# The prologue of a two-layer graph network on one core: degree count, row statistics and scaling in another order, with small operations moved between engines

## The chip, the cores and the metric

The kernel runs on one core of a Trainium2 chip. The metric is the time on the device in microseconds (us), from the first to the last instruction and what lies around them. Timed runs are given as a median; one further execution was taken with the hardware profiler, and everything that is said of single instructions comes from that one.

## The reference

`x` has 12,500 rows of 256 float32 values; an edge list of 200,000 pairs (`src`, `dst`) is sorted by `dst`. Two blocks follow one another:

```python
h = relu(layernorm(x))                       # mean and variance of each row
# block 1: two graph convolutions on the edges and a loop at every node
deg  = segment_sum(1, dst) + 1
dinv = rsqrt(deg)
conv(h, W, b) = segment_sum((h @ W)[src] * dinv[src] * dinv[dst], dst) + b
x = x + relu(conv(relu(conv(h @ W_pre + b_pre, W1, b1)), W2, b2)) @ W_post + b_post
# block 2: an attention layer in which node n mixes four heads of row dst[n]
x = x + attention(relu(layernorm(x)))
```

Because the weights can be multiplied after the sum over edges, the kernel gathers rows `relu(layernorm(x)) * dinv`, sums them by `dst`, and multiplies the sums by `W_pre @ W1`.

## The kernel before

Everything that runs is in `fast_path` (L414); `general_path` is a fallback for edge lists that are far from even, and is branched over here. Instructions keep the order in which the program emits them, engine by engine: there is no planner that moves them, so an instruction that waits holds back all that was emitted behind it on its engine. Semaphores are made by the language from the tiles that are read and written.

The 98 tiles of 128 rows (`NT`) are handled in 14 groups of seven (`NG`, `G`). The program has four stages.

**The prologue** (L506 to L870) makes `table1` in device memory: the rows `relu((x - mean) * rstd) * dinv`, with `dinv` in column 256. Its parts are:

- `load_edges` (L534) brings `dst` and `src` into 112 partitions of 1792 edges, `load_x` (L560) one group of x (896 KB). Eleven groups have buffers of their own (`XB`); the last three take the buffers of groups 0 to 2 once these have been written out (L823).
- The weights are multiplied on the PE (L670 to L688), and ACT copies each product out of PSUM.
- `near`, the offset of each `dst` within its neighbourhood, is made on DVE (L619), turned on the PE and copied out by ACT as `near_t` (`turned`, L699). `to_t` and `src_t` are made in the same way from `fto_f` (L634, L719) and `fsrc_f` (L723).
- `mean`, `off`, `ok` and `keeps` (L645 to L667) are a dozen one-column operations on POOL and one on DVE. They check that the edges are even enough and give the offsets of the later sums.
- The degree count runs over 16 blocks, four, four, four, three and one for the five parts `k`. `count_block` (L728) makes a one-hot `hot_r` on DVE (two buffers) and counts it with small matmuls. At the end of a part, `place` (L746) copies the counts (ACT, L750), makes a second one-hot `hot_n` (DVE, L753), multiplies both (PE, L759), copies the result (ACT, L773) and spreads it over partitions (PE, L778, 16 matmuls).
- `stats` (L781) takes mean and variance of a group: seven `bn_stats`, seven `bn_aggr` on DVE, one square root on ACT.
- `norms` (L790) turns the degrees of a part into `dinv`, and makes for all its rows the scale `sc` and the shift `nb` on DVE. Parts hold 3, 3, 4, 3 and 1 groups.
- `scale` (L806) writes one group in place, seven ACTIVATEs on ACT, or, with `both`, four on ACT and three pairs of operations on DVE; POOL copies `dinv` into column 256 (L810); SP starts the write to `table1` (L821).

What sets the order is the loop at L828: each block is followed by the statistics of the next group, then `place`, `norms` of the part before and one `scale` where they are due. After the loop the last groups are scaled with `both`.

**The first convolution** (`convolve`, L920, called at L1127) gathers 1563 tiles of 128 edges with indirect DMAs that POOL issues (L1077), and sums them on the PE with one-hots (L1082). **The second convolution** (L1235) does the same with `table2`. **The attention** (L1245 on) gathers its rows and writes the output. None of the three is touched by the change.

Of the kernel before, what the change touches and what calls it, by code (L numbers as in the profile page):

```python
# [413 lines left out]
def fast_path(  # L414
# [91 lines left out]
    with tc.tile_pool(name="fprep", bufs=1) as prep:  # L506
# [26 lines left out]

        def load_edges(e, pad, name):  # L534
            t = prep.tile([NCH, CE], I32, name=name)
# [24 lines left out]
        def load_x(g):  # L560
            n0, n1 = g * G * P, min((g + 1) * G * P, N)

            xt = prep.tile([P, G, D1], F32, name="fxt", bufs=XB)
# [11 lines left out]
        for g in range(XB):  # L575
            load_x(g)
            if g == 1:
                src_r = load_edges(src, 0, "fsrc_r")
# [39 lines left out]
        near = prep.tile([NCH, CE], F32, name="near_f")  # L618
# [9 lines left out]
        for k, q in enumerate(Q):  # L628
# [4 lines left out]
        to_f = prep.tile([NCH, CE], F32, name="fto_f")  # L633
        nc.vector.tensor_scalar(to_f, dst_r, base, None, op0=ALU.subtract)  # L634

# [6 lines left out]

        mean = prep.tile([NCH, 1], F32, name="fmean")  # L645
        nc.gpsimd.iota(mean, pattern=[[0, 1]], base=-LAG, channel_multiplier=M,
                       allow_small_or_imprecise_dtypes=True)
        nc.gpsimd.tensor_scalar(mean, mean, 0.0, None, op0=ALU.max)
        mean_i = prep.tile([NCH, 1], I32, name="mean_i")
        nc.gpsimd.tensor_copy(mean_i, mean)  # L650
        nc.vector.tensor_scalar(mean_i, mean_i, ~(P - 1), None, op0=ALU.bitwise_and)
        off = prep.tile([NCH, 1], F32, name="off")
        nc.gpsimd.tensor_copy(off, mean_i)
        nc.gpsimd.tensor_scalar(off, off, float(P * NT), None, op0=ALU.min)
        nc.gpsimd.tensor_sub(off, base, off)


        ok = prep.tile([NCH, 2], F32, name="ok")
        nc.gpsimd.tensor_sub(keeps[:, 1:2], mean, base)
        nc.gpsimd.tensor_scalar(keeps[:, 0:1], keeps[:, 1:2], 0.0, None, op0=ALU.is_le)  # L660
        nc.gpsimd.tensor_scalar(keeps[:, 1:2], keeps[:, 1:2], float(NL), float(P), op0=ALU.add,
                                op1=ALU.min)
        nc.gpsimd.tensor_scalar(ok[:, 0:1], off, 0.0, None, op0=ALU.is_ge)
        nc.gpsimd.tensor_scalar(ok[:, 1:2], off, float(OFF), None, op0=ALU.is_le)
        for i in range(2):
            nc.gpsimd.tensor_mul(keeps[:, 0:1], keeps[:, 0:1], ok[:, i:i + 1])
        nc.gpsimd.tensor_scalar(off, off, 0.0, float(OFF), op0=ALU.max, op1=ALU.min)  # L667
# [22 lines left out]
        with tc.tile_pool(name="fpsum", bufs=2, space=PSUM) as psum, \  # L690
# [28 lines left out]
            turned(to_f, to_t.rearrange("p c j -> p j c"), by_act)  # L719
            src_f = prep.tile([NCH, CE], F32, name="fsrc_f")  # L720

            def turn_src():
                nc.scalar.activation(src_f, src_r, AF.Copy)  # L723
                turned(src_f, src_t.rearrange("p c j -> p j c"), by_act)
# [21 lines left out]
            def place(k):  # L746
# [4 lines left out]
                hot = prep.tile([I, L * max(AW)], BF16, name="hot_n", bufs=2)  # L751
                hot = hot[:rows, :L * aw].rearrange("i (l a) -> i l a", a=aw)
                nc.vector.tensor_tensor(hot, a_bf[:rows, k, :, None].to_broadcast([rows, L, aw]),  # L753
                                        iota_a[:rows, :, :aw], ALU.is_equal)
# [26 lines left out]
            def stats(g):  # L781
                w0 = g * G
                st = prep.tile([P, G, 6], F32, name="fstats", bufs=2)
                for i in range(G):
                    nc.vector.bn_stats(st[:, i, :], xs[g][:, i, :D])
                for i in range(G):
                    nc.vector.bn_aggr(mv[:, w0 + i, :], st[:, i, :])
# [573 lines left out]
```

## Time and profile before

| what | us |
|---|---|
| median of 3 timed runs | 4939.63 (4938.75 to 4964.09) |
| the profiled execution, its own time | 4244.97 |
| its span, first to last instruction | 4243.1 |
| start to first gather of the first convolution | 126.47 |
| first to last gather of the second convolution | 2106.23 to 4070.28 |
| POOL busy, PE busy, DVE busy, ACT busy over the span | 3102.3, 3275.7, 1116.3, 409.1 |

The profiled execution took 694.7 us less than the median of the timed runs. Busy times are sums over the span; the timeline gives the start and length of each instruction or run of like instructions, with the engine's idle time before it and what ended it in brackets. Lines of the profile name an instruction by engine, source line, operation, and output and input tiles.

### The profile page before, as it was taken

What the parts mean: (1) busy time and instruction counts of PE and PEld (TensorE: products, weight loads), DVE (VectorE), ACT (ScalarE), POOL (GpSimd) and SP (SyncE); (2) the same over time, 40 slices, a digit from 0 to 9 for tenths busy, and PEclk for the clock granted to TensorE, in tenths of its full rate; (3) what the DMA queues carried; (4) which work ended last, traced back from release to release, by engine and by line L of the source; (5) the groups of instructions that cost most, each with busy time, mean ns of one, the idle gap of its engine ahead of it and who ended that gap; (6) DMA issues with size and microseconds to landing.
All of it is one profiled execution on the core that took longest, in us unless ns stands there. A gap on an engine that the chain in (4) does not pass through costs nothing. (4 is left out here: it accounts for less than half of the span.)

```text
span 4243.1 us, 32312 instructions
## 1 busy us (share of the span) xinstructions
PE 3275.7 (77%) x10867; PEld 2000.0 (47%) x10867; DVE 1116.3 (26%) x2257; ACT 409.1 (10%) x1066; POOL 3102.3 (73%) x3304
## 2 busy tenths in 40 slices
PE   6587878877887788788678877777878877877773
PEld 5244444434444444444345545555555554555552
DVE  8322222122222222222122222222222222222238
ACT  4100000000000000000001111111111111111122
POOL 2677777777777777777677777777777777777766
PEclk7678787788777777877778898998788888888886
DMA  6544444444444444444445444444444444444456
GB/s 212 159 121 119 119 119 121 119 118 120 121 119 119 119 121 119 119 119 120 124 124 135 127 123 124 127 124 123 124 126 125 124 124 126 126 123 124 124 157 186
DMA packets 300154, 543.46 MB, mean 128 GB/s; under 512 B 83149, under 2 KB 198604, under 8 KB 299980
## 3 DMA queue, kind: packets, MB, share of 16 engines
q0 software_dynamic: 153520, 414.27, 36.7%
q1 hardware_dynamic: 115014, 111.19, 8.4%
q10 hardware_dynamic: 31446, 15.83, 1.3%
q8 instruction: 90, 1.47, 0.1%
q14 instruction: 84, 0.69, 0.1%
HBM read 488.00 MB, written 52.93 MB: 127 GB/s over the span
## 5 line engine op out<-in xcount | busy, mean ns | idle before, releaser
L1077 POOL DMA_INDIRECT fgot<-ftable,fsrc_t x3126 | 2978.4, 953 | 985.1 <-issue 954.1
L1082 PE MATMUL facc<-fgot,fhot 128*128 128x257 f32 (+1 forms) x6252 | 2365.7, 496 | 788.6 <-DMA fgot<-ftable,fsrc_t 749.8
L1082 PEld LDWEIGHTS facc<-fgot,fhot 128*128 128x128 f32 x6252 | 1215.9, 228 | 1798.4 <-DMA fgot<-ftable,fsrc_t 1462.9
L1028 DVE TENSOR_TENSOR buf<-buf,fturn 128x256 f32 x224 | 94.5, 422 | 1677.4 <-PE fturn L972 1645.0
L1005 DVE TENSOR_TENSOR fhot<-iota_p,to_t 128x1792 f32<-128x1792 f32 x224 | 448.3, 2003 | 0.1
L1166 DVE SCALAR_TENSOR_TENSOR fx<-fpo,fdinv,fxb 128x256 f32<-128x256 f32 x97 | 47.0, 484 | 1301.5 <-PE fpo L1162 1301.5
L1012 ACT ACTIVATE fsums<-facc 128x257 f32<-128x257 f32 (+1 forms) x224 | 86.4, 386 | 1352.3 <-PE facc L1082 1348.5
L1111 PE MATMUL fpo<-wf,buf 128*128 128x256 f32 x388 | 157.6, 551 | 0.4 <-DVE buf L1028 0.4
L1149 PE MATMUL fpz<-buf,fwb 128*128 128x128 f32 x776 | 145.1, 316 | 0.0
L1272 POOL DMA_INDIRECT fal<-table_l,fsrc_t x98 | 94.8, 967 | 50.9 <-issue 27.4
L1111 PEld LDWEIGHTS fpo<-wf,buf 128*128 128x128 f32 x388 | 114.9, 297 | 29.3 <-DVE buf L1028 0.7
L1149 PEld LDWEIGHTS fpz<-buf,fwb 128*128 128x128 f32 x776 | 120.3, 219 | 14.9 <-issue 2.9
L1116 ACT ACTIVATE fo<-fpo,fdinv 128x256 f32<-128x256 f32 x97 | 46.0, 474 | 791.7 <-PE fpo L1112 791.7
L972 PE MATMUL fturn<-fident,self 128*128 128x128 f32 x396 | 87.8, 309 | 35.5 <-DMA self<-ftable 33.7
L1161 PE MATMUL fpo<-fwo,fz 128*128 128x256 f32 x388 | 111.2, 411 | 0.0
L1151 PE MATMUL fpz<-rm,fb2r 1*128 1x128 f32 x388 | 102.0, 345 | 0.0
L972 PE MATMUL fturn<-fident,fsums 128*128 128x128 f32 x448 | 99.5, 309 | 0.5 <-ACT fsums L1012 0.5
L1263 PE MATMUL fends<-rows,hot_t 128*128 128x260 f32 x196 | 68.6, 526 | 38.9 <-ACT fxg L1265 38.7
L1044 DVE COPY buf<-buf 128x640 f32<-128x640 f32 x194 | 97.6, 503 | 3.3
L972 PEld LDWEIGHTS fturn<-fident,fsums 128*128 128x128 f32 x448 | 72.8, 163 | 34.4 <-issue 11.5
L1112 PE MATMUL fpo<-bb,fins 2*128 2x256 f32 x194 | 86.1, 530 | 0.0
L972 PEld LDWEIGHTS fturn<-fident,self 128*128 128x128 f32 x396 | 58.8, 164 | 43.9 <-issue 35.7
(205 smaller groups left out, 1590.0 us busy)
## 6 DMA issues: line engine op xcount, KB each, us to landing
fgot<-ftable,fsrc_t POOLq DMA_INDIRECT x3126
ftable<-fxt SPq DMA_DIRECT2D x14, 910.0 KB
self<-ftable SPq DMA_DIRECT2D x97, 130.0 KB
ftable<-fo ACTq DMA_DIRECT2D x98, 128.0 KB
kept_x<-fx SPq DMA_DIRECT2D x98, 128.0 KB
fxr<-kept_x SPq DMA_DIRECT2D x14, 896.0 KB
self<-ftable SPq DMA_DIRECT2D x97, 128.0 KB
fxb<-in_x_dram SPq DMA_DIRECT2D x97, 128.0 KB
```

Source lines behind the costliest of these rows:

```text
L972: nc.tensor.transpose(v["pt"][:, i * KC + k, :], rows[:, k * P:(k + 1) * P], ident)
L1005: nc.vector.tensor_tensor(h[:, :n, :], iota_p[:, None, :].to_broadcast([P, n, P]), to_t[:, c, :n, None].to_broadcast([P, n, P]), ALU.is_equal)
L1012: nc.scalar.activation(sb, acc, AF.Copy)
L1028: nc.vector.tensor_add(b, b, v["pt"][:, :KC, :])
L1044: nc.vector.tensor_copy(nxt[:, :, :BW - P], buf[:, :, P:])
L1077: nc.gpsimd.indirect_dma_start(out=got, out_offset=None, in_=table[:], in_offset=bass.IndirectOffsetOnAxis(ap=src_t[:, c, j:j + 1], axis=0))
L1082: nc.tensor.matmul(acc, hots[c][:, j, :], got[:, :width], start=(j == 0), stop=(j == nj[c] - 1))
L1111: nc.tensor.matmul(po, buf[:, k, :P], wf[:, k, :], start=(k == 0), stop=False)
L1149: nc.tensor.matmul(pz[:, m, :], wb[:, k, m * P:(m + 1) * P], buf[:, k, :P], start=(k == 0), stop=False)
L1151: nc.tensor.matmul(pz[:, m, :], b2r[:, m * P:(m + 1) * P], v["rm"], start=False, stop=True)
L1161: nc.tensor.matmul(po, v["z"][:, m, :], wo[:, m, :], start=(m == 0), stop=False)
L1272: nc.gpsimd.indirect_dma_start(out=al[:, i, :], out_offset=None, in_=table_l[:], in_offset=bass.IndirectOffsetOnAxis(ap=src_t[:, c, j:j + ...
```

## The change

All of it is in the prologue:

- Statistics of one group follow only every second block of the degree count (and group 0's come first, ahead of the weight products); the last five groups' statistics follow the loop, each with the scaling of one group.
- The reciprocal of a group's standard deviation is taken per group (`flip`), between the `bn_stats` and the `bn_aggr` of the next group.
- The scale `sc` and the shift `nb` are made per group of seven columns on POOL, inside `scale`, with three operations; before, DVE made them per part with two.
- `deg` is copied out of PSUM by ACT, not DVE.
- The second one-hots `hot_n` of all five parts are made on POOL ahead of the loop, each by a subtraction and a comparison with zero.
- `to_f` and its turning move from before the loop to behind the first block.
- Groups 11 to 13 of x get a pool of their own in the place of the edge rows, and are loaded once `src` has been turned (behind block 1), not when a written group gives its buffer.
- The block of `mean`, `off`, `ok`, `keeps` moves from ahead of the weight products to behind the scaling, ahead of the gathers.
- `norms` is due two blocks after its `place`; while the loop and the rounds of statistics run, `scale` uses ACT alone; `both` is left for groups that remain after that.

```diff
+        edges = ExitStack()
+        rows_p = edges.enter_context(tc.tile_pool(name="frows", bufs=1))
-            t = prep.tile([NCH, CE], I32, name=name)
+            t = rows_p.tile([NCH, CE], I32, name=name)
...
-        to_f = prep.tile([NCH, CE], F32, name="fto_f")
-        nc.vector.tensor_scalar(to_f, dst_r, base, None, op0=ALU.subtract)
...
-        mean = prep.tile([NCH, 1], F32, name="fmean")
-        nc.gpsimd.iota(mean, pattern=[[0, 1]], base=-LAG, channel_multiplier=M,
-                       allow_small_or_imprecise_dtypes=True)
...
+        flipped = set()
+        def flip(g):
+            if g not in flipped:
+                flipped.add(g)
+                nc.vector.reciprocal(sc[:, g * G:(g + 1) * G], sc[:, g * G:(g + 1) * G])
+        def stats(g):
+            w0 = g * G
+            st = prep.tile([P, G, 6], F32, name="fstats", bufs=2)
+            for i in range(G):
+                nc.vector.bn_stats(st[:, i, :], xs[g][:, i, :D])
+            if g:
+                flip(g - 1)
+            for i in range(G):
+                nc.vector.bn_aggr(mv[:, w0 + i, :], st[:, i, :])
+            nc.scalar.activation(sc[:, w0:w0 + G], mv[:, w0:w0 + G, 1], AF.Sqrt, bias=eps)
+        stats(0)
         with tc.tile_pool(name="wpsum", bufs=2, space=PSUM) as psum:
...
-            turned(to_f, to_t.rearrange("p c j -> p j c"), by_act)
-            src_f = prep.tile([NCH, CE], F32, name="fsrc_f")
+            hot_n = []
+            for k, q in enumerate(Q):
+                h = prep.tile([I, L * max(AW)], BF16, name="hot_n", bufs=NPT)
+                h = h[:J * q, :L * AW[k]].rearrange("i (l a) -> i l a", a=AW[k])
+                nc.gpsimd.tensor_sub(h, iota_a[:J * q, :, :AW[k]],
+                                     a_bf[:J * q, k, :, None].to_broadcast([J * q, L, AW[k]]))
+                nc.gpsimd.tensor_scalar(h, h, 0.0, None, op0=ALU.is_equal)
+                hot_n.append(h)
+            def turn_to():
+                to_f = rows_p.tile([NCH, CE], F32, name="fto_f")
+                nc.vector.tensor_scalar(to_f, dst_r, base, None, op0=ALU.subtract)
+                turned(to_f, to_t.rearrange("p c j -> p j c"), by_act)
...
-                nc.vector.tensor_tensor(hot, a_bf[:rows, k, :, None].to_broadcast([rows, L, aw]),
-                                        iota_a[:rows, :, :aw], ALU.is_equal)
+                hot = hot_n[k]
...
-                nc.vector.tensor_scalar(deg[:, w0:w1], parts[k][:, :w1 - w0], 1.0, None,
-                                        op0=ALU.add)
+                nc.scalar.activation(deg[:, w0:w1], parts[k][:, :w1 - w0], AF.Copy, bias=1.0)
                 nc.scalar.activation(root[:, w0:w1], deg[:, w0:w1], AF.Sqrt)
-                nc.vector.reciprocal(sc[:, w0:w1], sc[:, w0:w1])
                 nc.vector.reciprocal(dinv[:, w0:w1], root[:, w0:w1])
-                nc.vector.tensor_mul(sc[:, w0:w1], sc[:, w0:w1], dinv[:, w0:w1])
-                nc.vector.scalar_tensor_tensor(nb[:, w0:w1], mv[:, w0:w1, 0], -1.0, sc[:, w0:w1],
-                                               op0=ALU.mult, op1=ALU.mult)
...
+                ws = slice(g * G, (g + 1) * G)
+                flip(g)
+                nc.gpsimd.tensor_mul(sc[:, ws], sc[:, ws], dinv[:, ws])
+                nc.gpsimd.tensor_mul(nb[:, ws], mv[:, ws, 0], sc[:, ws])
+                nc.gpsimd.tensor_scalar(nb[:, ws], nb[:, ws], -1.0, None, op0=ALU.mult)
...
-                if g + XB < NG:
-                    load_x(g + XB)
-            stats(0)
+            n_stats, due = 1, []
             for s, (k, j0) in enumerate(blocks):
                 count_block(k, j0)
-                if s + 1 < NG:
-                    stats(s + 1)
+                if s % 2 == 0:
+                    stats(n_stats)
+                    n_stats += 1
                 if j0 + JB[k] >= J:
                     place(k)
-                if k and (j0 == JB[k] or JB[k] >= J):
-                    norms(k - 1)
+                    due.append((s + 2, k))
+                if due and due[0][0] == s:
+                    norms(due.pop(0)[1])
+                if s == 0:
+                    turn_to()
                 if s == 1:
                     turn_src()
-                if to_scale:
-                    scale(k == NPT - 1)
-            norms(NPT - 1)
+                    edges.close()
+                    more = edges.enter_context(tc.tile_pool(name="fmore", bufs=1))
+                    for g in range(XB, NG):
+                        load_x(g, more)
+                if to_scale and to_scale[0] < n_stats:
+                    scale(False)
+            while n_stats < NG or due:
+                if n_stats < NG:
+                    stats(n_stats)
+                    n_stats += 1
+                if due:
+                    norms(due.pop(0)[1])
+                if to_scale and to_scale[0] < n_stats:
+                    scale(False)
             while to_scale:
                 scale(True)
             nc.vector.reciprocal(dinv2, deg)
+        edges.close()
+        mean = prep.tile([NCH, 1], F32, name="fmean")
...
```

## The prediction

> **What bounds the kernel now.** I read the page's groups first, then busy times by stretches of 20 us, then the timelines of all engines up to the first gather. The chain of waits reaches back only some 20 us from the end, and says nothing here.
>
> From the page, the group of the gathers:
>
> ```profile
> L1077 POOL DMA_INDIRECT fgot<-ftable,fsrc_t x3126 | 2978.4, 953 | 985.1 <-issue 954.1
> ```
>
> The 3126 gathers of both convolutions take (2978.4 + 985.1)/3126 = 1.27 us each, back to back. POOL's issue paces everything behind the first gather, and the change touches nothing there. So the change is worth what it does to the time of the first gather. POOL's timeline:
>
> ```profile
> 107.53 0.20 POOL L810 COPY fxt<-fdinv 128x7 f32<-128x7 f32 x1 [3.36 <-DVE fdinv L798]
> 126.47 1.24 POOL L1077 DMA_INDIRECT fgot<-ftable,fsrc_t  x1 [18.75 <-issue]
> ```
>
> The first gather waits for the last write of the first table. The stretches (columns: stretch, its length, then busy us and count of PE, PEld, DVE, ACT, POOL, then granted clock, DMA share, GB/s) show who sets that:
>
> ```profile
> 20.00:40.00 20.00, 15.64 (x86) 12.19 (x86) 20.00 (x73) 8.92 (x16) 1.51 (x9) 0.63 1.09 352
> 40.00:60.00 20.00, 12.63 (x79) 10.30 (x79) 19.71 (x63) 8.62 (x21) 0.19 (x1) 0.74 0.15 52
> 60.00:80.00 20.00, 13.90 (x79) 11.63 (x79) 19.71 (x63) 11.93 (x29) 1.36 (x9) 0.72 0.64 188
> 80.00:100.00 20.00, 15.45 (x102) 13.15 (x103) 15.98 (x37) 13.78 (x34) 0.59 (x4) 0.67 0.70 229
> 100.00:120.00 20.00, 6.80 (x36) 5.18 (x34) 14.06 (x50) 13.67 (x31) 0.66 (x4) 0.50 0.74 249
> ```
>
> DVE is full from 20 to 90 us; PE is at two thirds to three quarters beside it; POOL has nothing to do. From DVE's timeline, its one long wait and the first count block behind it:
>
> ```profile
> 18.94 0.15 DVE L651 TENSOR_SCALAR mean_i<-mean_i 112x1 int32<-112x1 int32 x1 [4.03 <-POOL mean_i L650]
> ...
> 21.78 2.00 DVE L734 TENSOR_TENSOR hot_r<-near_t,iota_r 128x3584 bf16<-128x3584 bf16 x1
> ```
>
> From PE's, counting at two speeds (16 matmuls each) and the last count:
>
> ```profile
> 53.84 3.15 PE L742 MATMUL tiles<-hot_r,slide 128*56 128x224 bf16 x16 [3.66 <-DVE hot_r L734]
> ...
> 74.50 2.09 PE L742 MATMUL tiles<-hot_r,slide 128*56 128x224 bf16 x16 [1.19 <-DVE hot_r L734]
> ...
> 102.05 0.57 PE L759 MATMUL count<-hot_n,tiles_b 14*32 14x55 bf16 x7 [0.50 <-ACT tiles_b L750]
> ```
>
> From ACT's, the last scalings, and from SP's, the last writes and the read that waits for them:
>
> ```profile
> 107.07 9.92 ACT L819 ACTIVATE fxt<-fxt,fnb,fsc 128x256 f32<-128x256 f32 x20
> ```
>
> ```profile
> 79.86 38.21 SPq L821 DMA_DIRECT2D ftable<-fxt  x11
> 125.60 6.94 SPq L966 DMA_DIRECT2D self<-ftable  x4
> ```
>
> The last count ends at 102.6, ACT and DVE together scale the last groups until 117.5, the last write starts at 117.7 and has landed by 125.6. That is the path: DVE, then a short counting tail, then scaling on two engines, then 7.9 us for a backlog of writes.
>
> **What the Trainium skill says.** "GPSIMD Engine Reference", section Performance versus the Vector engine, gives a two-input elementwise operation of 2048 float32 as 4497 ns on POOL against 2293 on DVE, 2.2 ns an element; its Key points add that POOL shares its SBUF interfaces with DVE, and that a DVE instruction with two SBUF inputs contends. This trace has only small POOL operations of two inputs: low_q took 278 ns with 56 columns and 209 with 14, so 1.64 ns an element. It does show the contention, the same select of `sel` (L609) at 2.77 us beside DVE's near_f and 1.08 us alone. "TensorE: Matmul & The Clock Gate", The HAM clock gate, says that an idle PE falls to half clock and needs some 3.4 us of work to recover. The trace agrees: the clock is 0.50 from 105 to 125, where PE hardly works, and up to 1.00 in other short stretches. "Perfetto Trace Analysis", Tensor Engine Instruction, says that ACT and DVE are strict first-in, first-out. The trace has ACT's instructions in emitted order throughout.
>
> **The change part by part**, against the profiled execution (4244.97 us; span 4243.1).
>
> 1. Head. DVE loses its 4.0 us wait for POOL (mean_i, L651) and to_f (1.3 us) ahead of the loop, so stats(0) runs from 13.6 (where base ends now) for 2.85, to 16.45. But its square root now stands ahead of the weight copies on ACT, which now start at 4.62. They are held until 16.8; behind ACT wait PE's weight products, and behind those PE's turning of near. From the first weight copy to the first copy of near_t there are 3.6 us of products, 1.0 for the bias, 0.6 of zeros and 1.2 for turning and copy, with hand-offs 6.9; a PE idle since 5 us adds about 2. The first hot_r starts at 25.5, not at 21.8: **+3.7**. Bounds: 23.6 with PE at full clock, 28 with PE at half clock throughout.
>
> 2. Counting. DVE's load per two blocks falls from 9.6 us (two hot_r of 2.0, two stats of 2.9) to 6.95. Over 16 blocks DVE has 28.7 (hot_r) + 8 x 2.95 + 1.3 = 53.6 us, against 75 before. So DVE no longer sets the pace; PE does. Sixteen counting matmuls took 3.15 us where the clock was near 0.5 to 0.7 and 2.09 where it was near 0.8 to 0.9; I take 2.7. PE's sum: 224/16 x 2.7 = 37.8, four spreadings of 16 (1.93 to 3.61) at 2.7 = 10.8, the products of L759 5.3, turning to and src 6.1: 60.0. Hand-offs to ACT in the five `place` come to about 1.5 each (tiles_b 0.35, counted 0.6 and twice the wait for a semaphore), 7.5, and some 2.5 more where tiles_b stands behind a scale (3.55 us) on ACT. PE starts when a_bf is done, 3.1 + 3.3 after near's turning begins, at 30.8. The last count ends at 30.8 + 60.0 + 7.5 + 2.5 = **100.8**, against 102.6. The freed 21 us of DVE buy 2. What was DVE's wait is now PE's; hot_n's part of it (PE waited 7.5 us for it) is in this sum.
>
> 3. Scaling. In the loop it is ACT alone, a group at s = 5, 6, 7, 9, 10, 11, 13, 14, 15: nine groups. Group 0 starts at 53.2: the fourth block ends at 46.3, place takes it to 51.3, deg, root, reciprocal and four POOL operations of 0.2 another 1.9. That is 1.3 us behind 51.9 now. Group 8 ends at 104.8 (from 101.2, behind the last counted). Five groups then remain with statistics not yet made, where before two engines finished at 2.0 us a group. A round is now in series: square root 0.3 (it waits on ACT behind the scale before), reciprocal on DVE 0.2, three POOL operations and a copy 0.9 with their gaps, seven ACTIVATEs 3.55: **5.0 us**; stats (2.9) lies beside ACT. Deg and root of part 3, emitted behind group 8, and its reciprocal, flip and POOL put the first round's ACTIVATEs at 107.0 to 110.6. The second carries norms of the last part too and ends at 116.4, then 121.4, 126.4, **131.4**. The work of `both`, 18 tiles on DVE, is gone: no group is left for it.
>
> 4. Last write. It starts at 131.5. With writes 5 us apart there is no backlog: the lone first write took from 55.55 to 60.08, 4.5 us. Landed at 136.0, and the first gather 0.9 behind it as now: **136.9, against 126.5: +10.4 us**.
>
> 5. Edits that I cost at nothing. hot_n on POOL: 6272 columns, at 1.64 to 2.2 ns for the subtraction and 1.0 (iota_a: 1.52 us for 1526) for the comparison 17 to 20 us, with contention up to 29; it starts at 28, and the idle POOL hides it until group 0's `sc` at 52.4. The three x loads, their POOL memsets and their SP issues stand behind it, and SP's first table write (56.9) behind them; their data is wanted only at 112. The moved mean block is 3.6 us of POOL and one DVE step; POOL reaches it at 127.7 and is done at 131.5, under the last write; the DVE and PE steps that need `off` take 3.6 more, to 135.1. If the write landed 4 us sooner they would show. deg on ACT: 0.2 us five times, in the times above.
>
> Span 4253.5, profiled execution 4255.4. The median of the timed runs is 694.7 us above the profiled one, and no view here shows where that lies; I carry the difference over: 4939.6 + 10.4 = **4950**. Half a per cent, about what a measurement of this kernel can tell from no change, is 24.7 us: 4915 to 4964.
>
> **Rivals.**
>
> - A warm PE. Denser counting keeps the clock near 1.0: 14 x 2.1 + 4 x 1.93 + 4 + 5 + 7.5 = 54 us of counting, so the last count ends by 85. ACT is then the bound: 47 + nine groups of 4.0 to 83, then five rounds of 5.0 and the tail parts to 113, landing 117.5, gather at 119: 7 us gained, **4932**. For it: 0.84 to 1.00 appear in some 5 us stretches where PE works. Against: PE still has gaps at each place.
> - Slower than before, by POOL. If POOL's one-hots run at the 2.5 times that L609 showed for their whole length, they take 20.7 x 2.5 = 52 us and end at 80. Group 0's scale and shift then wait from 53 to 80, tiles_b(1) stands behind that scale on ACT, PE behind tiles_b: 27 us for all that follows, gather at 164, **4977**. It decides from the point where POOL's one-hots need over 25 us; each us beyond shows, and 14 more carry the loss over half a per cent. For it: POOL has no larger two-input operation to measure by. Against: DVE's two-input operations are under half of its time.
> - A cold PE in the timed runs. At half clock counting costs 14 x 0.45 + 4 x 0.9 = 10 us more, of which before, bound by DVE, saw little: **4960**.
> - The change does nothing that shows: that is the first case's size in the measurement.
>
> **How the numbers follow.** Forecast, 4940 to 4960: 0.50. Warm PE, 4926 to 4940: 0.18. Cold PE, 4956 to 4968: 0.14. POOL, 4964 to 4985: 0.14. A gain of over 24.7 us needs the first gather before 101.8, when even the warm case gives 119: no step here gives that, and 0.04 is left for what I have not seen. Slower by over half a per cent: POOL's 0.14 and a third of the cold case, 0.19; same 0.77; faster 0.04. The range 4930 to 4968 leaves out some 0.07 below and 0.12 above.
>
> **What would show it.** First gather near 137. ACT's square root near 16.5 with the weight copies behind it, first hot_r near 25. DVE idle in the loop, waiting for hot_r's buffers. POOL's one-hots 3 to 5 us a part, done by 57. Five scalings at the end with 1.4 us of idle ACT before each, writes 5 us apart. The forecast is wrong if the last count ends before 90, if ACT waits for POOL at group 0, or if the gathers' 1.25 us changes.

## The result, and the profile after

| what | before | after |
|---|---|---|
| median of 20 timed runs each, us | 4946.17 (4924.30 to 4971.49) | 4975.97 (4961.08 to 4992.44) |
| ratio of the two, 95% interval | | 1.0055 [1.0042, 1.0068] |
| span of the profiled execution, us | 4243.1 | 4976.5 |
| start to first gather in it, us | 126.47 | 151.63 |

The changed kernel is slower by 0.55%, 27 us (21 to 34). The forecast was 4950 with a range up to 4968; the time lies above it.

The two spans in this table must not be compared. The gathers' group of the changed kernel:

```profile
L1114 POOL DMA_INDIRECT fgot<-ftable,fsrc_t x3126 | 2971.1, 950 | 1601.9 <-issue 942.8
```

A gather takes as long as before (950 ns), but the idle time ahead of the gathers went from 985.1 to 1601.9 us. That looks like a huge loss, and it is none of the change's: the changed kernel with a single memset moved (one of the experiments below) ran in another session with this group at

```profile
L1114 POOL DMA_INDIRECT fgot<-ftable,fsrc_t x3126 | 2982.8, 954 | 972.4 <-issue 935.5
```

and a median of 4269.03. The kernel before gave a median of 4247.87 on that chip and one of 4951.17 on a further chip. So these programs run at one of two paces, near 4250 or near 4950 us, and the pace was the same for all that ran on one chip; whether the chip or something else sets it was not tried. The profile of before had the quick pace and its timed runs the slow one, which is where the 694.7 us come from that the prediction carried over without a place. By the two profiles they lie behind the first gather: from there to the end it took 4116.6 us before and 4824.9 after. POOL stops there for 533.2 us in the profile of the changed kernel, in 135 stops whose end the profile cannot name, and PE, which sums the gathered rows, waits 18.3 us for them where it waited 749.8. So the prediction's "POOL's issue paces everything behind the first gather" holds at the quick pace; what holds POOL at the slow one is open.

Ratios below are always taken on one chip, and profiles are compared by their first gather: 126.47 and 127.96 in two profiles of before, both quick, and 151.63 and 151.57 in two of the changed kernel, both slow. No kernel was profiled at both paces, so it is not shown directly that the prologue has no part in this. But POOL's first four steps for the one-hots took 2.78, 4.08, 7.41 and 4.06 us at the quick pace and 2.78, 4.08, 7.41 and 4.07 at the slow one (in the two experiments with the memset on DVE). The 25.2 us between 126.47 and 151.63 are 0.51% of 4946, and the measured 0.55% agrees with that within its interval.

Where the 25.2 us come from shows in POOL's timeline (start, length, engine, line, operation, then idle time before it and what ended it):

```profile
25.86 2.78 POOL L719 TENSOR_TENSOR hot_n<-iota_a,a_bf 56x1526 bf16<-56x1526 bf16 x1 [8.42 <-ACT a_bf L712]
28.73 4.08 POOL L721 TENSOR_SCALAR hot_n<-hot_n 56x1526 bf16<-56x1526 bf16 x1
32.80 7.41 POOL L719 TENSOR_TENSOR hot_n<-iota_a,a_bf 56x1526 bf16<-56x1526 bf16 x1
40.30 4.06 POOL L721 TENSOR_SCALAR hot_n<-hot_n 56x1526 bf16<-56x1526 bf16 x1
...
60.32 1.46 POOL L721 TENSOR_SCALAR hot_n<-hot_n 14x504 bf16<-14x504 bf16 x1
...
62.38 0.09 POOL L772 MEMSET counted<- 32x1 f32 x1
```

The second one-hots fill POOL from 25.86 to 61.78, 35.9 us for ten instructions; then come the memsets of the last x tiles, and then a memset of one column, 0.09 us long. PE's timeline shows who needs it:

```profile
47.09 0.87 PE L764 MATMUL count<-hot_n,tiles_b 56*32 56x218 bf16 x7 [0.44 <-POOL hot_n L719]
62.53 3.60 PE L783 MATMUL fdegs<-counted,sel 64*128 64x21 f32 x16 [14.57 <-POOL counted L772]
```

`place(0)` has its product at 48.0 and its counts copied by ACT at 48.6, and PE stands idle for 14.57 us until POOL has reached that memset. The other twelve blocks stand behind it on PE. In the kernel before, the same memset was long done when PE came to it:

```profile
21.79 0.09 POOL L767 MEMSET counted<- 32x1 f32 x1
...
42.93 1.93 PE L778 MATMUL fdegs<-counted,sel 64*128 64x21 f32 x16 [0.79 <-ACT counted L709]
```

The stretches of all engines, which for before had DVE at 20.00, 19.71 and 19.71 of 20, now read (columns as before):

```profile
40.00:60.00 20.00, 7.07 (x48) 5.22 (x46) 12.58 (x26) 4.30 (x9) 19.74 (x7) 0.67 0.42 132
60.00:80.00 20.00, 13.52 (x79) 11.29 (x79) 11.00 (x35) 8.19 (x19) 6.27 (x19) 0.67 0.21 71
```

From 40 to 60 POOL is the full engine (19.74), with seven instructions; PE, DVE and ACT wait for it. From ACT's timeline, the head, the first scaling and the last:

```profile
16.35 0.30 ACT L660 ACTIVATE fsc<-fmv,feps 128x7 f32<-128x7 f32 x1 [14.06 <-DVE fmv L659]
16.56 0.64 ACT L672 ACTIVATE wpt<-fw 128x256 f32<-128x256 f32 x2
...
67.98 3.55 ACT L815 ACTIVATE fxt<-fxt,fnb,fsc 128x256 f32<-128x256 f32 x7 [1.37 <-POOL fnb L805]
...
142.34 3.55 ACT L815 ACTIVATE fxt<-fxt,fnb,fsc 128x256 f32<-128x256 f32 x7 [1.17 <-POOL fnb L805]
```

Group 0 is scaled from 67.98 (forecast 53.2), the last group until 145.9 (131.4), and the gather follows 5.7 us later at 151.63 (136.9). The three misses are 14.8, 14.5 and 14.7 us, about the size of the one stall of PE at 48.

### The profile page after: what moved, and what is told of

Read it like the earlier page. It is cut to its first block, busy times and chain, and to the rows that moved or that the text cites. A ratio compares the mean times of both kernels' runs of the same rounds, so it can differ in the third digit from the quotient of the medians.

```text
span 4976.5 us, 32328 instructions
## 1 busy us (share of the span) xinstructions
PE 2941.8 (59%) x10867; PEld 2200.5 (44%) x10867; DVE 1105.1 (22%) x2210; ACT 413.0 (8%) x1089; POOL 3143.9 (63%) x3356
## 4 chain that ended last, share of the span: by engine, by line
another core or an unknown queue 39%; POOL 28%; issue 14%; DVE 8%; PE 7%; ACT 2%; DMA 1%; DVEq 0%; ACTq 0%; SPq 0%; POOLq 0%
POOL fgot L1114 27%; PE facc L1119 3%; DVE fhot L1042 3%; DVE fx L1203 1%; DVE st L1207 1%; DVE buf L1065 1%; DVE buf L1081 1%; PE fpz L1186 1%; PE fpo L1198 1%; ACT fxt L815 0%; PE fpz L1188 0%; DVE buf L1085 0%; PE fturn L1009 0%; DMA table_l<-fxa 0%
## 5 line engine op out<-in xcount | busy, mean ns | idle before, releaser
L1114 POOL DMA_INDIRECT fgot<-ftable,fsrc_t x3126 | 2971.1, 950 | 1601.9 <-issue 942.8
L1119 PE MATMUL facc<-fgot,fhot 128*128 128x257 f32 (+1 forms) x6252 | 1898.1, 451 | 456.9 <-issue 434.4
L1119 PEld LDWEIGHTS facc<-fgot,fhot 128*128 128x128 f32 x6252 | 1367.6, 228 | 822.4 <-issue 574.0
L1148 PE MATMUL fpo<-wf,buf 128*128 128x256 f32 x388 | 132.2, 474 | 355.6 <-DVE buf L1065 312.2
L1224 PE MATMUL fpt<-fident,h 128*128 128x128 f32 x194 | 60.5, 411 | 467.9 <-DVE sc L1214 246.7
L1148 PEld LDWEIGHTS fpo<-wf,buf 128*128 128x128 f32 x388 | 86.2, 234 | 402.2 <-issue 389.2
L1224 PEld LDWEIGHTS fpt<-fident,h 128*128 128x128 f32 x194 | 26.9, 187 | 502.8 <-issue 298.4
L1186 PE MATMUL fpz<-buf,fwb 128*128 128x128 f32 x776 | 192.6, 394 | 0.0
L1198 PEld LDWEIGHTS fpo<-fwo,fz 128*128 128x128 f32 x388 | 74.0, 210 | 262.7 <-ACT fz L1193 222.5
L1186 PEld LDWEIGHTS fpz<-buf,fwb 128*128 128x128 f32 x776 | 159.9, 285 | 19.5 <-issue 15.0
L1188 PE MATMUL fpz<-rm,fb2r 1*128 1x128 f32 x388 | 135.5, 444 | 0.0
```

Of the source, the lines that this page charges most:

```text
L1114: nc.gpsimd.indirect_dma_start(out=got, out_offset=None, in_=table[:], in_offset=bass.IndirectOffsetOnAxis(ap=src_t[:, c, j:j + 1], axis=0))
L1119: nc.tensor.matmul(acc, hots[c][:, j, :], got[:, :width], start=(j == 0), stop=(j == nj[c] - 1))
L1148: nc.tensor.matmul(po, buf[:, k, :P], wf[:, k, :], start=(k == 0), stop=False)
L1186: nc.tensor.matmul(pz[:, m, :], wb[:, k, m * P:(m + 1) * P], buf[:, k, :P], start=(k == 0), stop=False)
L1188: nc.tensor.matmul(pz[:, m, :], b2r[:, m * P:(m + 1) * P], v["rm"], start=False, stop=True)
L1198: nc.tensor.matmul(po, v["z"][:, m, :], wo[:, m, :], start=(m == 0), stop=False)
```

## The experiments

The theory after this reading: POOL's queue is the cause. Its one-hots end at 62 instead of 48, and two things stand behind them in order, first the memset of `counted`, then the scale and shift of group 0. The rival: the memset alone is the accident, and the rest of POOL's work is hidden. A second rival: POOL costs DVE so much through their common access to SBUF, the on-chip memory, that DVE's delay, not the queue, makes the loss. A third: the head and the tail of the new schedule cost more than forecast.

**Before once more**, unchanged, as a control.

> The kernel before, unchanged. If the prologue runs at a fixed pace, the first gather starts at 126.5 us again whatever the span is, and the 25.2 us by which the changed kernel's first gather is later (151.6) are the change's own. If the span is near 4940 instead of 4243 and the gathers stand longer than 1.27 us apart, the short span of the first profile lies behind the first gather and has nothing to do with the change. Ratio to the kernel before: 1.000, and its interval shows what can be told from no change.

Median 4245.87, ratio 0.9996 [0.9988, 1.0005], first gather 127.96. The prologue has its first gather within 1.5 us of the first profile's, so differences of first gathers below some 1.5 us say nothing.

**The memset of `counted` on DVE**, all else as changed:

```diff
-                    nc.gpsimd.memset(cs[R:, 0:1], 0.0)
+                    nc.vector.memset(cs[R:, 0:1], 0.0)
```

> The changed kernel with one word changed: the memset of one column of the first counted tile is on DVE, not on POOL. Theory, a small operation stuck in POOL's queue: PE waited 14 us for it, because it stood behind five one-hots and four memsets of x tiles. First gather 151.6 - 13.5 = 138 us, about 1.0025 of the kernel before. Rival, the one-hots on POOL cost the time themselves, by holding DVE's operations: PE is released, but the loop stays slow, first gather at 147 or later, 1.004 or more.

A miss: first gather 147.54, ratio 1.0049 [1.0035, 1.0062]. PE's wait is gone, as its timeline shows:

```profile
48.27 3.48 PE L783 MATMUL fdegs<-counted,sel 64*128 64x21 f32 x16 [0.70 <-ACT counted L704]
```

but ACT's first scaling hardly moved:

```profile
66.77 3.55 ACT L815 ACTIVATE fxt<-fxt,fnb,fsc 128x256 f32<-128x256 f32 x7 [14.54 <-POOL fnb L805]
```

The wait of 14.57 on PE has become one of 14.54 on ACT: the next thing that POOL owes, group 0's shift `nb`, stood in the same place of the same queue. POOL's one-hots even end later, at 65.35 and not at 61.78, with DVE at work beside them. So the rival of the lone memset falls. A queue that is late is late for all that is behind it, and taking out its first victim uncovers the second.

**Both taken off POOL**: the memset, and scale and shift (`sc`, `nb`) on DVE, while POOL keeps the one-hots. What is left of POOL's one-hots is their contention with DVE. DVE makes scale and shift in two steps, where POOL made them in three.

```diff
-                    nc.gpsimd.memset(cs[R:, 0:1], 0.0)
+                    nc.vector.memset(cs[R:, 0:1], 0.0)
...
-                nc.gpsimd.tensor_mul(sc[:, ws], sc[:, ws], dinv[:, ws])
-                nc.gpsimd.tensor_mul(nb[:, ws], mv[:, ws, 0], sc[:, ws])
-                nc.gpsimd.tensor_scalar(nb[:, ws], nb[:, ws], -1.0, None, op0=ALU.mult)
+                nc.vector.tensor_mul(sc[:, ws], sc[:, ws], dinv[:, ws])
+                nc.vector.scalar_tensor_tensor(nb[:, ws], mv[:, ws, 0], -1.0, sc[:, ws],
+                                               op0=ALU.mult, op1=ALU.mult)
```

> The changed kernel with all that waits for POOL's queue moved off it: the one-column memset is on DVE, and the scale and the shift of a group are made on DVE; the one-hots stay on POOL. Theory, queue: what is left of the one-hots is that POOL and DVE hold each other up while they last, the 4.7 us by which the first part's count came later with them (46.7) than without (42.0). First gather 134.7 + 4.5 = 139 us. Rival, contention is the larger part: 144 or later.

First gather 138.50, ratio 1.0008 [0.9991, 1.0024]. Against 151.57 of the changed kernel, run once more on the same chip, 13.1 us are gone. Not all of that is POOL's queue. With two steps in the place of three, the last five scalings follow one another in 18.0 us (first start 111.24, last 129.25), where the changed kernel's take 20.0 (122.35 to 142.34). The last count of each lies ahead of that tail. The changed kernel's, and this one's:

```profile
115.93 0.57 PE L764 MATMUL count<-hot_n,tiles_b 14*32 14x55 bf16 x7 [0.44 <-ACT tiles_b L758]
```

```profile
105.28 0.55 PE L764 MATMUL count<-hot_n,tiles_b 14*32 14x55 bf16 x7 [0.44 <-ACT tiles_b L758]
```

By these ends, 116.5 and 105.8, the difference is 10.7 us, and up to 1 us of it is a head that happened to be sooner (first `hot_r` at 23.08, not 24.03). So POOL's queue is worth some 10 to 13 us.

**The changed kernel once more**, the other end of that comparison:

> The changed kernel itself, beside the kernel before on one chip. First gather 151.6 us again, 24 to 25 us behind the kernel before; ratio 1.0055 to 1.006 if the whole loss lies ahead of the first gather. Rival, part of it lies in the convolutions: ratio above 1.007 with the same first gather.

Median 4980.64, ratio 1.0062 [1.0040, 1.0085], first gather 151.57.

**The one-hots back on DVE**, made inside `place` as before; memset, scale and shift stay on POOL, all else as changed:

```diff
...
-                nc.gpsimd.tensor_sub(h, iota_a[:J * q, :, :AW[k]],
-                                     a_bf[:J * q, k, :, None].to_broadcast([J * q, L, AW[k]]))
-                nc.gpsimd.tensor_scalar(h, h, 0.0, None, op0=ALU.is_equal)
...
-                hot = hot_n[k]
...
+                nc.vector.tensor_tensor(hot, a_bf[:rows, k, :, None].to_broadcast([rows, L, aw]),
+                                        iota_a[:rows, :, :aw], ALU.is_equal)
```

> The changed kernel with the second one-hots back on DVE inside place, as before; the memset stays on POOL, with nothing but the memsets of x tiles ahead of it. Theory, queue: POOL is free when the memset comes, so first gather near 138 us, plus what PE waits for hot_n on DVE (up to 7 us over five parts), less the 4 to 8 us by which POOL's one-hots held DVE: 135 to 143. Rival, the late tail and the head alone make the loss and the one-hots do not matter: 150.

First gather 134.66, 0.3 us below the expected span, ratio 1.0021 [1.0012, 1.0030]: with this one part undone, 17 of the 25 us are gone. It is also the schedule of the forecast with the one-hots elsewhere than on POOL (DVE makes all five in 7.2 us), so it shows how good the rest of the working was. Its last count, and its last scaling and first gather:

```profile
98.93 0.55 PE L758 MATMUL count<-hot_n,tiles_b 14*32 14x55 bf16 x7 [0.43 <-ACT tiles_b L749]
```

```profile
125.32 3.55 ACT L809 ACTIVATE fxt<-fxt,fnb,fsc 128x256 f32<-128x256 f32 x7 [1.17 <-POOL fnb L799]
...
134.66 1.25 POOL L1108 DMA_INDIRECT fgot<-ftable,fsrc_t  x1 [5.75 <-DMA self<-ftable]
```

The ends are 99.5, 128.9 and 134.7 where the forecast had 100.8, 131.4 and 136.9. From the memset, scale and shift moved (138.50) to the one-hots moved (134.66) there are 3.8 us at the first gather, and 6.4 at the last count (105.8 to 99.5), ahead of the two tails. Part of the 6.4 can be the scale and shift that DVE carries in the one run only, and the two profiles are from two chips. So contention costs some 4 to 7 us, net of what DVE gains by having no `hot_n` to make: the second rival has its share, and it is the smaller one.

**Only the one-hots, into the kernel before**: the opposite test, with the changed kernel's loop over the five parts ahead of the count.

```diff
...
+                nc.gpsimd.tensor_sub(h, iota_a[:J * q, :, :AW[k]],
+                                     a_bf[:J * q, k, :, None].to_broadcast([J * q, L, AW[k]]))
+                nc.gpsimd.tensor_scalar(h, h, 0.0, None, op0=ALU.is_equal)
...
-                nc.vector.tensor_tensor(hot, a_bf[:rows, k, :, None].to_broadcast([rows, L, aw]),
-                                        iota_a[:rows, :, :aw], ALU.is_equal)
+                hot = hot_n[k]
```

> The kernel before with one part of the change alone: the second one-hots of all five parts on POOL ahead of the loop. Theory, queue: the one-column memset of the first counted tile stands behind 34 us of one-hots here too, from about 20 to 55 us, so PE's spreading of the first part starts at 55 instead of 42.9; DVE then waits for the buffers of hot_r, and the first gather is 8 to 13 us later, at 135 to 140, 1.002 to 1.003 of the kernel before. Rival: the one-hots on POOL free 7 us of DVE, which is full there, and the first gather comes 3 to 7 us sooner, at 120 to 123.

First gather 136.45, ratio 1.0022 [1.0015, 1.0029]. The one part alone makes the kernel before slower by 9 us (8.5 at the first gather, against the control on the same chip), although it takes work off DVE, which is full there. The mechanism is the same, on PE:

```profile
57.63 3.60 PE L784 MATMUL fdegs<-counted,sel 64*128 64x21 f32 x16 [13.25 <-POOL counted L773]
```

**Two parts of five on POOL**: a smaller dose, so that POOL is done before `place(0)` needs it.

```diff
-            for k, q in enumerate(Q):
+            for k, q in enumerate(Q[:2]):
...
-                hot = hot_n[k]
+                if k < 2:
+                    hot = hot_n[k]
+                else:
...
+                    nc.vector.tensor_tensor(hot, a_bf[:rows, k, :, None].to_broadcast([rows, L, aw]),
+                                            iota_a[:rows, :, :aw], ALU.is_equal)
```

> The changed kernel with the second one-hots of the first two parts on POOL as in the change, those of the other three on DVE as before; the one-column memset and the scale and shift stay on POOL. Theory, queue: POOL is through its one-hots at 44 us, before the memset is wanted (48) and before group 0's scale is (53), so nothing waits for the queue, and only contention is left: first gather 134.7 + 3.8 = 138.5 us at most. Rival, every one-hot costs its share: half of the elements, half of the 16.9 us, 143.

First gather 138.79, ratio 1.0034 [1.0021, 1.0048]; 0.3 us over what my theory allowed and 4 under its rival. The one-hots end at 44.80, the memset runs at 45.41, and PE waits 0.79 us for ACT in its place: no queue loss. What stays, 4.1 us over the kernel without one-hots on POOL, is contention, but for up to 1 us of a head that happened to be later (first `hot_r` at 24.47, not 23.46). At the last count it is 4.2 us, or 3.2 without that head, where all five parts cost 6.4. So about half of the work (two of five `hot_n`, 3.5 of DVE's 7.2 us) costs half to two thirds of the contention, and nothing of the queue: that loss begins where POOL's work outlasts its deadline.

**The head undone**: from the kernel with one-hots on DVE, group 0's square root moves behind the weight copies on ACT.

```diff
+            if g:
+                root_of(g)
+
+        def root_of(g):
+            w0 = g * G
             nc.scalar.activation(sc[:, w0:w0 + G], mv[:, w0:w0 + G, 1], AF.Sqrt, bias=eps)
...
+            root_of(0)
```

`root_of(0)` stands behind the weight copies, the turning of `near` and the copies of `a_bf`.

> The changed kernel with the second one-hots on DVE, and the square root of group 0 behind the weight products on ACT, where nothing waits for it. Theory, head: the weight copies start near 4.6, near is turned by 14.3, and the first hot_r comes straight behind stats(0), at 16.4 instead of 23.5. The whole loop moves up by 7 us: first gather 134.7 - 7 = 127.7. Rival: later limits (loads of x, ACT) absorb the start, and the gain is under 2 us: 133 or later.

First gather 128.80, ratio 0.9992 [0.9973, 1.0010]. The weight copies start at 4.69 and not at 16.56, and the first `hot_r` moves up with them:

```profile
4.69 0.81 ACT L677 ACTIVATE wpt<-fw 128x256 f32<-128x256 f32 x2 [2.40 <-PE fw L675]
```

```profile
16.25 1.98 DVE L740 TENSOR_TENSOR hot_r<-near_t,iota_r 128x3584 bf16<-128x3584 bf16 x1
```

It starts at 16.25 against 23.46, and 5.9 of these 7.2 us arrive at the gather. A square root of 0.30 us had held the weight copies for 12.

**The tail changed**: from the same start, statistics after every block from the eighth on, and `both` after the loop.

```diff
-                if s % 2 == 0:
+                if s % 2 == 0 or s >= 7:
...
-                    scale(False)
+                    scale(True)
```

> The changed kernel with the second one-hots on DVE, with statistics after every block from the eighth on, so that all are made inside the loop, and with both ACT and DVE scaling after it. Theory, tail: the last count ends 2 to 4 us later, at 101 to 103 instead of 99.5, but the five groups left take 2.0 to 2.3 us each instead of 5.0: scaling ends near 117 instead of 128.9, a backlog of writes costs 2 to 3 us back, first gather 123 to 125. Rival, DVE is full again in the loop and the count ends as much later as the tail gains: 132 or later.

First gather 130.38, ratio 1.0008 [0.9993, 1.0022]: 4.3 us gained, less than expected. DVE is full again in the loop (19.30 and 19.29 of 20 us from 60 to 100), and the last count ends at 105.8, later than the 101 to 103 that I had put. Scaling ends at 123.1, and then another cover is gone:

```profile
130.38 1.25 POOL L1108 DMA_INDIRECT fgot<-ftable,fsrc_t  x1 [3.95 <-DVE root_t L899]
```

The gather waits for the chain behind the moved block of `mean` and `off` (POOL's `off` is done at 126.4, `root_t` at 129.9), not for the write. The prediction had named this cost and its cover: under the last write it is free, 4 us sooner it shows.

**A version with all of it mended**: one-hots on DVE, head undone, the block of `mean` on POOL behind block 2 in the loop, and statistics also at blocks 13 and 15; the last three groups' statistics in a row, then five groups with `both`. The loop's part of the edit, from the kernel with the head undone (`check_means` is the moved block):

```diff
-                if s % 2 == 0:
+                if s % 2 == 0 or s > 12:
...
-                    due.append((s + 2, k))
+                    due.append((s + 2 if k < 3 else s + 1, k))
...
+                if s == 2:
+                    check_means()
...
-                    scale(False)
-            while n_stats < NG or due:
-                if n_stats < NG:
-                    stats(n_stats)
-                    n_stats += 1
-                if due:
-                    norms(due.pop(0)[1])
-                if to_scale and to_scale[0] < n_stats:
-                    scale(False)
+                    scale(k == NPT - 1)
+            while n_stats < NG:
+                stats(n_stats)
+                n_stats += 1
+            norms(due.pop(0)[1])
```

> What the runs point to, together: one-hots on DVE; the square root of group 0 behind the weight products; statistics after every second block and after the last three, three groups behind the loop; norms of parts 3 and 4 one block after their place; both engines scaling from the last part on; the mean block behind the third block. First gather near 119 us, 8 ahead of the kernel before: ratio 0.998. Rival: the backlog of writes, 0.9 MB for each 2 us of scaling, takes most of it back: 124 or later, 0.9995.

A miss: first gather 129.93, ratio 1.0015 [1.0008, 1.0021]. The stretches say why; from 105 to 110 and from 115 to 120:

```profile
105.00:110.00 5.00, 0.00 (x0) 0.00 (x0) 5.00 (x28) 0.30 (x1) 1.12 (x7) 0.50 0.09 31
...
115.00:120.00 5.00, 0.00 (x0) 0.00 (x0) 3.85 (x14) 3.81 (x9) 0.79 (x4) 0.50 1.02 342
```

While DVE took three statistics in a row (5.00 of 5), ACT scaled nothing (0.30) and the DMA engines stood at 0.09. Then five groups were ready almost together, and their five writes of 910 KB went out at 342 GB/s, some 13 us, until about 129. By this reading the end was set by when the first of the last writes could start, not by when the last was ready. The next version tests it.

**The same with its tail in another order**: statistics of group 11 into DVE's wait at the last `place`, and ACT scaling groups 9 and 10 while DVE takes the last two.

```diff
+                if k == NPT - 1:
+                    stats(n_stats)
+                    n_stats += 1
...
             while n_stats < NG:
+                scale(False)
                 stats(n_stats)
                 n_stats += 1
-            norms(due.pop(0)[1])
+                if due:
+                    norms(due.pop(0)[1])
```

> The combined version of before (second one-hots on DVE, head undone, mean block in the loop) with its tail in another order: statistics of group 11 stand in DVE's 5 us wait behind the last one-hot, and groups 9 and 10 are scaled by ACT while DVE takes the last two statistics, instead of three statistics in a row with nothing scaled. My theory (in the combined version the DMA engines stood idle from 103 to 116.8 and then wrote five groups of 910 KB at some 350 GB/s until 129): the first write of these five starts at about 105, scaling ends near 115, first gather at 120 to 123, against 129.9, ratio to the kernel before 0.998 to 0.999. The rival, that the end is set by something that does not move with the order of the tail (the mean block, the read of the table): first gather at 128 to 130 again, ratio 1.000 to 1.002.

First gather 123.75, 0.75 us above the expected span; median 4243.43 against 4246.29, ratio 0.9990 [0.9982, 0.9999]. The stretch that was empty now has ACT and DMA at work beside DVE:

```profile
105.00:110.00 5.00, 0.35 (x1) 0.08 (x1) 4.05 (x24) 4.97 (x14) 1.61 (x8) 0.50 0.80 270
```

The empty stretch was the cause: the gather moved up by 6.2 us. This version is faster than the kernel before by 0.10%, 4 us (0.4 to 7.6), little above what the measurement can tell; the first gather, sooner by 2.7 and 4.2 us than in the two profiles of before, fits that. It was not run beside the changed kernel, whose ratio to before was 1.0055 and 1.0062.

## Why the prediction was wrong

**The step that failed is part 5**, "Edits that I cost at nothing": one-hots in 17 to 20 us, with contention up to 29, "and the idle POOL hides it until group 0's `sc` at 52.4". They took 35.9 us, and the first thing behind them that another engine wanted was due at 48, so PE waited 14.57 us. Three things in that sentence were off.

- The price. I took 1.0 ns an element for the comparison with a constant, from an `iota` of the same width. It took 4.08 us for 1526 elements, 3.22 for 1190 and 1.46 for 504, some 2.7 to 2.9 ns: dearer than the two-input subtraction in front of it (2.78 us, 1.8 ns, where I had 1.64 to 2.2). For 6272 elements that is 16.9 us, not 6.3. The Trainium skill, "GPSIMD Engine Reference", section Engine selection, calls an operation of one input on POOL roughly line-rate; in this trace it is half as dear again as one of two inputs, and the measurement decides. Subtractions of 11.4 and comparisons of 16.9 come to 28.3 us with nobody in the way, already the upper end of my span.
- The contention. Nearly all of the other 7.6 us of the 35.9 are POOL's waits for DVE: 4.7 in the second subtraction, 1.6 in the third comparison, 0.9 in the fourth subtraction. My 29 had no working of its own. The Trainium skill, "SBUF — State Buffer", section SBUF: two separate sides, which I had not used, gives a rule: POOL and DVE have one port pair in common, and the one that starts first holds it for its whole instruction while the other stops altogether; of DVE's instructions those in a two-port mode take part, and those with two SBUF inputs when POOL's instruction reads SBUF. The trace agrees with it in the main, and not throughout. DVE's timeline beside POOL's above:

```profile
28.81 4.95 DVE L726 TENSOR_SCALAR fto_f<-fdst_r,base 112x1792 f32<-112x1792 int32 x1
33.69 3.94 DVE L742 TENSOR_TENSOR hot_r<-near_t,iota_r 128x3584 bf16<-128x3584 bf16 x2
37.55 2.37 DVE L655 BATCH_NORM_STATS2 fstats<-fxt 128x6 f32<-128x256 f32 x7
...
40.52 3.93 DVE L742 TENSOR_TENSOR hot_r<-near_t,iota_r 128x1792 bf16<-128x1792 bf16 x1
...
51.71 2.19 DVE L742 TENSOR_TENSOR hot_r<-near_t,iota_r 128x3584 bf16<-128x3584 bf16 x1
```

  and a later step of POOL's:

```profile
47.15 5.72 POOL L721 TENSOR_SCALAR hot_n<-hot_n 56x1526 bf16<-56x1526 bf16 x1
```

  POOL's comparison runs from 28.73 to 32.81; DVE's `to_f`, 1.12 us where POOL is idle, starts at 28.81 and ends at 33.76, 0.95 after POOL is done. It has one input, and whether it runs in a two-port mode the trace does not tell. POOL's next subtraction starts at 32.80, stands through `to_f` and the two `hot_r` until 37.6, and then takes its 2.7: 7.41 in all. The `bn_stats` beside it take their 2.37 as ever. Two lines do not fit a full stop. The half `hot_r` at 40.52, 1.06 us alone, took 3.93, but it ends only 0.09 us after POOL's second comparison (40.30 + 4.06). The `hot_r` at 51.71 took 2.19 us, hardly more than alone, while POOL's comparison ran until 52.87. So the waits are shown; that the loser always stands still until the other is done is not.
- The deadline. I took group 0's `sc` at 52.4 as the first thing that POOL owes. It is the memset of one column of `counted`, emitted in `place(0)` and so behind all one-hots, and it is due at 48.0 to 48.6, when PE ends its last product (47.09 + 0.87) and ACT has copied the counts. I had counted the x memsets behind the one-hots and not this one. From the start of the one-hots at 25.86, POOL had 22 to 23 us, not 25. And my own upper end, 29 us from 28, lay at 57, behind even the deadline that I had; I put nothing down for it.

How these add up is an estimate from the figures above. One-hots of 20 us from 25.86 would have brought the memset to 46.5, in time even for the true deadline. At 28.3 us it would have come at 54.8, some 6 us late; the waits for DVE make that 62.4, some 14 late. So the price and the waits were the error that counted, and the missed memset is where it came in: without it the same queue made ACT wait 14.54.

Forecast and stall, 136.9 + 14.6, come to 151.5, against 151.63. This closes in part by luck. With the one-hots on DVE the same schedule had its gather at 134.66, 2.2 us sooner than forecast, and POOL's one-hots cost 17.0 us against that.

**The rival "slower than before, by POOL"** was the right mechanism with a wrong size: it had 52 us of one-hots and 4977 where 35.9 us and 4975.97 were measured. The near agreement of the times is partly luck: its 52 us are 2.5 times a sum of 20.7 that its own prices put at 20.1, its first gather was at 164, and the median of before also lay 6.5 us higher in 20 runs than in three. I gave it 0.14 against the argument that "DVE's two-input operations are under half of its time". That argument counts DVE's load over the whole loop; the one-hots lie in the stretch where `to_f` and the first `hot_r` come thick. And the range ended at 4968, under most of that rival's own 4964 to 4985.

**Step 1, head**: right in its mechanism, and a little too dear. The square root came at 16.35 (forecast 16.4), the first `hot_r` at 24.03 (25.5), and between 23.1 and 24.5 in other runs with the same head. Before, it came at 21.78, so the cost was some 2 us and not 3.7. Undoing the head gave more, 5.9 us at the gather, since the head of before had a 4.0 us wait of its own.

**Step 2, counting**: right, once POOL is out of it: 99.5 against 100.8, even with the five one-hots back on DVE, which the forecast did not have. PE sets the pace and DVE idles, so that the 21 us taken from DVE bought little.

**Step 3, scaling**: right. The last five scalings begin at 122.35, 127.62, 132.53, 137.43 and 142.34, 4.9 to 5.3 us apart (5.0), each with 1.2 to 1.3 us in which ACT waits for POOL's shift.

**Step 4, last write**: right. From the end of scaling to the gather 5.7 us (5.5).

**Rivals warm and cold PE**: the mean clock in the stretches of 20 us from 20 to 100 was 0.63 to 0.74 before and 0.67 to 0.72 after, between the two cases; neither came.

So the loss of 25 us, by first gathers: 17 by the one-hots on POOL, of which 10 to 13 are its queue and 4 to 7 its contention with DVE; 5.9 by the head; and 1 to 2, about what two profiles of one kernel differ by, for all the rest. The parts were undone in this one order; whether they add up in another was not tried.

## What to carry to other kernels

An idle engine is cover only up to its first deadline, and that can be the deadline of the smallest thing emitted behind the moved work: list every instruction of its queue in emitted order, memsets of one column too, and set each against the time at which its reader wants it. Before taking a long wait's last releaser away, look at what stands next in the releaser's queue; otherwise the wait only changes its victim. Work that is moved from DVE to POOL need not be out of DVE's way: here 7.6 of POOL's 35.9 us were waits for DVE, and DVE's own steps beside it took up to 4.4 times their length. Price such a move by an operation of the same kind and size, and add the waits of both sides.

## What the runs showed of the hardware

- The same program ran at one of two paces: the kernel before at a median of 4245 to 4248 us on three chips and of 4946 and 4951 in two other sets of runs, with the mean clock at 0.80 to 0.81 and 0.71 in the profiles of either kind. The idle time ahead of the 3126 gathers was 969 to 985 us in the quick profiles and 1587 to 1602 in the slow ones, which have POOL stopped for 484 to 533 us by something that the profile does not show. What sets the pace was not tried.
- POOL's bf16 comparison with a constant, in place, 2.7 to 2.9 ns an element for 504 to 1526 elements, against 1.8 to 2.0 for a two-input subtraction of the same tiles.
- Where POOL and DVE met, either one was held: `to_f` on DVE took 4.95 us beside a POOL comparison and 1.12 alone, and POOL's subtraction of 2.7 us took 7.41 behind `to_f` and two `hot_r`. Seven `bn_stats` took 2.37 us beside POOL as elsewhere.
- Small POOL steps were held as well: the shift's multiplication by -1, seven columns and 0.24 us alone, took 1.89 us beside a `hot_r`.
